# Shifting half of the features by one token: transfers in SBUF in place of products with a shift matrix (preLN mixed attention network, Trainium2)

## The chip, the cores and the metric

The kernel runs on one core of one Trainium2 chip. The core has five engines with a queue each: TensorE (PE, matrix products; PEld is its loading of the stationary operand), VectorE (DVE), ScalarE (ACT), GpSimd (POOL) and SyncE (SP, which here only issues transfers). Transfers run on 16 DMA engines beside them. Every engine works through its own queue in order and waits on semaphores for the others. The metric is the device time of one execution in microseconds.

## The reference

Eight sequences of 512 tokens with 256 features pass through four blocks: an attention with xPos rotation and a decaying product, a mixture of eight experts, a causal attention of 16 heads, and a stack of two local layers. Only the local layers are touched by the change. Cut to what matters:

```python
def shift_token(t):
    t1, t2 = jnp.split(t, 2, axis=-1)
    t2 = jnp.pad(t2, ((0, 0), (1, 0), (0, 0)))[:, :-1]
    return jnp.concatenate([t1, t2], axis=-1)

def _layer(x, wqkv, qs, ksc, wo, lg, lb, w1, b1, w2, b2):
    h = shift_token(x)
    ...                       # q, k, v; rotation; windows of 128 tokens
    x = x + o @ wo
    h = shift_token(x)
    mu = h.mean(-1, keepdims=True)
    var = h.var(-1, keepdims=True)
    h = (h - mu) / jnp.sqrt(var + 1e-05) * lg + lb
    h = h @ w1 + b1
    a, g = jnp.split(h, 2, axis=-1)
    h = a * jax.nn.gelu(g, approximate=False)
    return x + h @ w2 + b2
```

So each layer twice takes the second 128 features of every token from the token before it. The second of these shifts, the one ahead of the layernorm, is what the change is about.

## The kernel before

Rows of tokens lie on partitions. A sequence is a tile `x` of 128 partitions by 4 token tiles (t = 0 to 3) by 256 features in SBUF; all eight sequences stay there. All arithmetic is float32; each float32 product or transpose of the program is carried out as two matmul instructions, so counts in the trace are twice those of the code.

The local layers are written as 16 units (2 layers by 8 sequences). `Unit` has the steps: `flip` (transposes x to feature-major, the first shift is a change of one column there), `rows` (q and k of one token tile, with rotation), `value_rows`, `roots`, `turn` (normalise and transpose q and k), `scores`, `exponentials`, `weigh` (softmax of one token tile, four heads at a time), `flip_weights` (transposes the weights, `pt` to `pT`), `outputs` (`ov`), `project` (product with wo, and the sum into x, L997), `norm` (second shift and layernorm, L999 to L1028), `flip_normed` (transposes `hn`, L1030), `gated` (six chunks of the gated hidden layer) and `back` (product with w2, `fo`, and the sum into x at L1104).

The order is written out by hand in the loop at L1555. In iteration n the token tiles t = 0 to 3 of unit n (`u`) are attended; beside them stand steps of `ahead` (unit n+1: its flip, rows, turn), of `late` (unit n-1: norm, flip_normed, gated) and of `last` (unit n-2: back). `fill[t]` holds three lists of such steps: the first goes between `flip_weights(t)` and `outputs(t)`, the second between `outputs(t)` and the scores of the next token tile, the third behind `project(t)`. Matmuls and transposes of this part, and ACT's table loads and exponentials, keep their order of the program (`product`, L161; `transpose`, L165; `pinned`). DVE, POOL and SP get their order from the scheduler of the framework, which puts an instruction into its engine's queue where it expects it to become ready; semaphores are set by it too.

`norm` of the kernel before, at t = 0 in the first list:

```python
            sh = ps.tile([P, NT, P], F32, tag="ps", name="sh")
            for t in range(NT):
                product(sh[:, t, :], shift[:, 0, :], y[:, t, P:], start=True, stop=(t == 0))
                if t:
                    product(
                        sh[:, t, :], shift[:, 1, :], y[:, t - 1, P:], start=False, stop=True
                    )
```

`shift[:, 0]` is a matrix that moves every row one partition down, and `shift[:, 1]` one that moves the last row of the token tile before into row 0. That is 7 products per unit, into one PSUM buffer `sh` of the pool `ps` (three buffers, which `sh`, `fo`, `tp`, `qp`, `fp` and `tpq` take in turn). Statistics (L1012 to L1014) and normalisation (L1021) then read the first half of the features from x and the second from `sh`. ACT computes the inverse root as the exponential of a logarithm (L114).

SP issues in this part, in the kernel before, the loads of the second layer's weights (`wo`, `wf`, L738 to L747), and in the second layer per unit one load of the kept input (`x<-kept`, L1089) and one store of the result (`out_dram<-x`, L1106).

Of the kernel before, what the change touches and what calls it, by code (L numbers as in the profile page):

```python
# [10 lines left out]
F32 = mybir.dt.float32  # L11
# [8 lines left out]
P = 128  # L20
B, L, D = 8, 512, 256
NT = L // P
# [30 lines left out]
def forward_kernel(  # L53
# [22 lines left out]
    w2: bass.AP,  # L76
    b2: bass.AP,
    c_ident: bass.AP,
    c_shift: bass.AP,
    c_mask: bass.AP,  # L80
    c_rank: bass.AP,
    c_order: bass.AP,
# [8 lines left out]
    nc = tc.nc  # L91
# [51 lines left out]
    def layernorm(xb, dst):  # L143

        mv = moments(xb)
        standard(xb, dst, mv, rstd_of(mv, NT))
# [14 lines left out]
    def product(*args, **kw):  # L161

        tc.keep_in_program_order(nc.tensor.matmul(*args, **kw))  # L163
# [31 lines left out]
    with ExitStack() as st:  # L195
        pr1 = st.enter_context(tc.tile_pool(name="pA3", bufs=1, side="right"))
        pr2 = st.enter_context(tc.tile_pool(name="pA4", bufs=2, side="right"))
        ps = st.enter_context(tc.tile_pool(name="psA", bufs=6, space=PSUM))
# [11 lines left out]
        xs = [load_rows(0)]  # L210
# [25 lines left out]
        class Sequence:  # L236
# [6 lines left out]
            def norm(self):  # L243
                self.xn = p1.tile([P, NT, D], F32, tag="xn", name="xn")
                layernorm(xs[self.b][:, :, 1, :], self.xn)
# [232 lines left out]
        for b in range(B):  # L478
            keep = tc.keep_in_program_order
            for t in range(NT):  # L480
# [8 lines left out]
                last = (b, t - 1) if t else (b - 1, NT - 1)  # L489
# [19 lines left out]
                if b < 4 and t % 2 == 1:  # L509
# [3 lines left out]
                            out=w2_all[:, e].rearrange("p (f d) -> p f d", f=NF),  # L513
                            in_=ew2[e].rearrange("(f p) d -> p f d", p=P),
                        )
                    )
            if b == 2:
                keep(
                    nc.sync.dma_start(
                        out=rows_out.rearrange("(p s) d -> p s d", s=NS),  # L520
                        in_=c_zero[:, :D].unsqueeze(1).to_broadcast([P, NS, D]),
# [11 lines left out]
    with ExitStack() as st:  # L533
# [8 lines left out]
        number, steps = slots[0:1, :NS], slots[:, NS : NS + 32]  # L542
# [49 lines left out]
        start = chosen(need[0:1, :ne], "start")  # L592
# [110 lines left out]
        ahead = None  # L703
        for s in range(NS):
# [4 lines left out]
            ahead = (s, hT, g, c2, r)  # L709
# [8 lines left out]
    xs = [xpool.tile([P, NT, D], F32, tag=f"x{b}", name=f"x{b}") for b in range(B)]  # L718

    kept = [dram.tile([P, NT * D], F32, tag=f"kept{b}", name=f"kept{b}") for b in range(B)]  # L720
    wl = ctx.enter_context(tc.tile_pool(name="wl", bufs=1))
    masks = wl.tile([P, L + 2 * P], F32, name="masks")
    nc.sync.dma_start(out=masks, in_=c_mask)
    causal, window = masks[:, :L], masks[:, L:]
    shift = wl.tile([P, 2, P], F32, name="shift")
    rope2 = wl.tile([P, NT, 4, DH2], F32, name="rope2")
    lng_sb = wl.tile([P, DEPTH, NC], F32, name="lng_sb")
    lnb_sb = wl.tile([P, DEPTH, NC], F32, name="lnb_sb")
# [20 lines left out]

    wqkv_of = [load_qkv(0, wl)]  # L750
    layer = load_layer(0)
    nc.sync.dma_start(out=shift, in_=c_shift)
    nc.sync.dma_start(out=rope2, in_=c_rope2)
    nc.sync.dma_start(out=lng_sb, in_=lng)
    nc.sync.dma_start(out=lnb_sb, in_=lnb)
# [55 lines left out]
    class Unit:  # L811
# [172 lines left out]
        def project(self, t):  # L984
# [11 lines left out]
            y = xs[self.b][:, t, :]  # L996
            nc.vector.tensor_tensor(y, pr[:, :D], y, ALU.add)  # L997

        def norm(self):  # L999

            y = xs[self.b]
            sh = ps.tile([P, NT, P], F32, tag="ps", name="sh")
            for t in range(NT):
                product(sh[:, t, :], shift[:, 0, :], y[:, t, P:], start=True, stop=(t == 0))
                if t:
                    product(
                        sh[:, t, :], shift[:, 1, :], y[:, t - 1, P:], start=False, stop=True
                    )
            mv = lnp.tile([P, NT, 2], F32, tag="mv", name="mv")
            for t in range(NT):  # L1010
                sta = lnp.tile([P, 2, 6], F32, tag="st2", name="st2", bufs=4)
                nc.vector.bn_stats(sta[:, 0, :], y[:, t, :P])  # L1012
                nc.vector.bn_stats(sta[:, 1, :], sh[:, t, :])
                nc.vector.bn_aggr(mv[:, t, :], sta.rearrange("p a b -> p (a b)"))  # L1014
            exponentials_next()
            rstd = lnp.tile([P, NT], F32, tag="rstd", name="rstd")
            inverse_root(rstd, mv[:, :, 1], pinned=True, bias=eps)
            self.hn = d1.tile([P, NT, D], F32, tag="hn", name="hn")
            for t in range(NT):
                for c, src in enumerate((y[:, t, :P], sh[:, t, :])):  # L1020
                    nc.vector.tensor_scalar(  # L1021
                        self.hn[:, t, c * P : (c + 1) * P],
                        src,
                        mv[:, t, 0:1],
                        rstd[:, t : t + 1],
                        ALU.subtract,
                        ALU.mult,
                    )  # L1028
# [84 lines left out]
    ps = ctx.enter_context(tc.tile_pool(name="psC", bufs=3, space=PSUM))  # L1113
# [5 lines left out]
    with ExitStack() as st:  # L1119
# [373 lines left out]
        for slot in range(max(max(fill) + 1, END + 3)):  # L1493
            steps = []
            if slot < END:
                n, i = divmod(slot, UNITS)
# [6 lines left out]
            n, i = divmod(slot - 3, UNITS)  # L1503
# [7 lines left out]
            n, i = divmod(slot, UNITS)  # L1511
# [8 lines left out]
    with ExitStack() as st:  # L1520
        d1 = st.enter_context(tc.tile_pool(name="pD1", bufs=1))
        d2 = st.enter_context(tc.tile_pool(name="pD2", bufs=2))
        psb = st.enter_context(tc.tile_pool(name="psDb", bufs=2, space=PSUM))
        psa = st.enter_context(tc.tile_pool(name="psDa", bufs=1, space=PSUM))

        wqkv_of.append(load_qkv(1, d1))

        uT = d1.tile([P, NFC, L], F32, name="uT")
        nc.vector.memset(uT[:, NFC - 1, :], 1.0)

        qT = d1.tile([P, H2 // 2, L], F32, name="qT")
        kT = d1.tile([P, H2 // 2, L], F32, name="kT")

        def unit(n):
            return units[n] if 0 <= n < len(units) else None

        def steps(u, *names):

            return [(getattr(u, name), args) for name, *args in names] if u else []

        u = units[0]
        for t in range(NT):
            u.turn(t)
            if t == 0:
                for quad in range(2):
                    u.scores(0, quad)
                for quad in range(2):
                    u.exponentials(0, quad)
        for quad in range(2):
            u.weigh(0, quad)  # L1550

        for n in range(len(units) + 2):  # L1555
            u, ahead, late, last = unit(n), unit(n + 1), unit(n - 1), unit(n - 2)
            fill = [
                [
                    steps(late, ("norm",)) + steps(last, ("back", 0)),
                    steps(last, ("back", 1)) + steps(ahead, ("flip",)),  # L1560
                    steps(last, ("back", 2))
                    + steps(ahead, ("rows", 0, 0))
                    + steps(last, ("back", 3))
                    + steps(ahead, ("rows", 0, 1))
                    + steps(late, ("flip_normed",)),
                ],
                [
                    steps(late, ("gated", 0), ("gated", 1)),
                    steps(ahead, ("value_rows", 0)),
                    steps(ahead, ("rows", 1, 0), ("rows", 1, 1), ("rows", 2, 0)),  # L1570
                ],
                [
                    steps(late, ("gated", 2), ("gated", 3)),
                    [],
                    steps(ahead, ("rows", 2, 1), ("rows", 3, 0), ("rows", 3, 1)),
                ],
                [
                    steps(ahead, ("roots",)) + steps(late, ("gated", 4), ("gated", 5)),
                    steps(ahead, *(("turn", t) for t in range(NT))),
                    steps(ahead, *(("value_rows", t) for t in range(1, NT))),  # L1580
                ],
            ]
            for t in range(NT):
                then, at = (u, t + 1) if t + 1 < NT else (ahead, 0)
                if u:
                    u.flip_weights(t)
                for do, args in fill[t][0]:
                    do(*args)
                if u:
                    u.outputs(t)  # L1590
                for do, args in fill[t][1]:
                    do(*args)
                if then:
                    for quad in range(2):
                        then.scores(at, quad)
                    for quad in range(2):
                        then.exponentials(at, quad)
                if u:
                    u.project(t)
                rest = fill[t][2]  # L1600
                for i, (do, args) in enumerate(rest):
                    do(*args)
                    if i < 2 and then:
                        then.weigh(at, i)
                if then:
                    for i in range(len(rest), 2):
                        then.weigh(at, i)
            if u and u.b == B - 1 and u.l + 1 < DEPTH:
                layers.append(load_layer(u.l + 1))
# [3 lines left out]
def _constants():  # L1613
    f = np.float32
    ident = np.eye(P, dtype=f)


    shift = np.zeros((P, 2, P), f)
    shift[np.arange(P - 1), 0, np.arange(1, P)] = 1
    shift[P - 1, 1, 0] = 1  # L1620

# [32 lines left out]
    i, j = np.arange(2 * NT - 1)[None, :, None], np.arange(P)[None, None, :]  # L1656
# [24 lines left out]

    return {
        "c_ident": ident,
        "c_shift": shift,
        "c_mask": mask,
        "c_rank": rank,
        "c_order": np.ascontiguousarray(order),
# [73 lines left out]
```

## Time and profile before

| what | us |
|---|---|
| median of 3 runs (lowest, highest) | 2668.21 (2662.66, 2675.25) |
| profiled execution, its own time | 2658.87 |
| its span, first to last instruction | 2657.2 |
| PE busy (share of the span) | 2501.0 (94%) |
| DVE, ACT, POOL busy | 1553.7, 1123.8, 464.0 |
| local layers: first and last `sh` start | 1328.5, 2608.0 |
| from one `sh` of the second layer's units to the next (1930.50 to 2017.58) | 87.1 |
| one matmul instruction of `sh`, and their number | 0.275, 224 |
| granted TensorE clock, mean of the span | 0.975 |

The page of the profile gives busy times by engine and by groups of instructions; a group's mean time of one matmul holds the part in which it overlaps the next. Where a matmul's share of the elapsed time is needed, the chain of waits has it, which counts every moment once. The timeline lists instructions in order of time with the idle time ahead of them and what released them; "<-issue" is a pause without a visible cause. The DMA view lists packets (one for each contiguous piece of a transfer, and small ones that signal its end), and issues with the median time from issue to landing.

### The profile page before, as it was taken

How to read it: one execution, taken by the hardware profiler on the slowest of the kernel's cores; microseconds unless marked ns; L12 is line 12 of the kernel's file. 1: busy time of each engine (PE TensorE's matmuls, PEld its weight loads, DVE VectorE, ACT ScalarE, POOL GpSimd, SP SyncE). 2: the span in 40 equal slices, each digit the busy share in tenths (PEclk: the TensorE clock that was granted, in tenths of full speed). 3: DMA queues.
4: the chain of work that ended last, by engine and by line, in shares of the span. 5: the costliest groups of instructions: out<-in, count | busy, mean ns of one | idle time of the engine just before them, and what ended most of it. 6: DMA issues, size and time to landing. Idle time of an engine off the chain costs nothing.

```text
span 2657.2 us, 39880 instructions
## 1 busy us (share of the span) xinstructions
PE 2501.0 (94%) x14590; PEld 1606.1 (60%) x14590; DVE 1553.7 (58%) x4763; ACT 1123.8 (42%) x2504; POOL 464.0 (17%) x632
## 2 busy tenths in 40 slices
PE   8998699996999999989899999999999999999998
PEld 5666688873444444444656666666666666666665
DVE  6665322224566666656676667567656766666653
ACT  2222111112444444434555555456545554555452
POOL 1322100003333333212110011001101111111100
PEclk9999799997999999979999999999999999999999
DMA  5620576633000000001000000000001000000000
GB/s 166 167 69 32 193 229 220 207 116 112 9 17 17 17 9 17 9 11 48 1 1 1 1 1 1 1 1 1 3 7 33 1 17 17 16 10 8 17 17 24
DMA packets 69495, 122.42 MB, mean 46 GB/s; under 512 B 11870, under 2 KB 47284, under 8 KB 69044
## 3 DMA queue, kind: packets, MB, share of 16 engines
q1 hardware_dynamic: 63700, 105.31, 12.4%
q0 software_dynamic: 4096, 12.59, 1.3%
q8 instruction: 117, 1.92, 0.3%
q10 hardware_dynamic: 1504, 1.97, 0.2%
q14 instruction: 78, 0.64, 0.1%
HBM read 97.96 MB, written 29.10 MB: 48 GB/s over the span
## 4 chain that ended last, share of the span: by engine, by line
PE 83%; DVE 8%; issue 3%; DMA 2%; ACT 2%; POOL 1%; SPq 0%; DVEq 0%; POOLq 0%; ACTq 0%
PE qp L163 12%; PE fp L163 11%; PE ov L163 9%; PE sc L163 8%; PE fo L163 7%; PE pr L163 7%; PE hp L668 6%; PE sd L163 5%; PE yp L691 4%; PE tpq L166 3%; PE pt L166 3%; PE qk L163 2%; PE tp L166 2%; DVE scrap L150 2%; PE vp L163 1%
## 5 line engine op out<-in xcount | busy, mean ns | idle before, releaser
L864 POOL TENSOR_TENSOR turned<-turned,turn 128x512 f32<-128x512 f32 x128 | 163.1, 1274 | 1105.6 <-DVE turn L856 1029.5
L163 PE MATMUL qp<-wqkv,xT 128*128 128x512 f32 x768 | 350.9, 599 | 0.1
L150 DVE CUSTOM_DVE_ANT_0 scrap<-sc,masks 128x256 f32<-128x256 f32 (+1 forms) x500 | 243.5, 487 | 171.5 <-PE sc L163 153.0
L163 PE MATMUL sc<-kT,qT 64*128 64x256 f32 (+2 forms) x2024 | 314.2, 429 | 13.8 <-DVE qrow L150 11.7
L163 PE MATMUL fp<-hT,wf 128*128 128x512 f32 (+1 forms) x704 | 313.8, 595 | 6.1 <-DVE hT L1040 6.1
L1311 ACT ACTIVATE pT<-sd 128x768 f32<-128x768 f32 (+1 forms) x192 | 169.1, 881 | 237.1 <-PE sd L163 117.1
L150 DVE CUSTOM_DVE_ANT_0 prob<-sc,masks 128x256 f32<-128x256 f32 (+1 forms) x512 | 164.4, 387 | 151.3 <-PE sc L163 151.3
L923 ACT ACTIVATE prob<-prob,nmax 128x256 f32<-128x256 f32 (+1 forms) x512 | 239.1, 468 | 24.0 <-DVE nmax L150 23.4
L163 PE MATMUL sd<-qA,kT 32*128 32x512 f32 (+3 forms) x1024 | 205.9, 494 | 31.8 <-ACT pT L1311 28.6
L163 PEld LDWEIGHTS qp<-wqkv,xT 128*128 128x128 f32 x768 | 141.6, 190 | 154.3 <-issue 135.2
L163 PEld LDWEIGHTS fp<-hT,wf 128*128 128x128 f32 (+1 forms) x704 | 128.3, 189 | 158.4 <-issue 139.8
L163 PEld LDWEIGHTS sc<-kT,qT 32*128 32x128 f32 (+1 forms) x2024 | 171.1, 190 | 72.3 <-DVE qrow L150 40.1
L163 PE MATMUL fo<-wf,uT 128*128 128x256 f32 (+1 forms) x768 | 190.4, 390 | 0.0
L680 DVE TENSOR_SCALAR hT<-hp,c 128x128 f32<-128x128 f32 x156 | 54.4, 349 | 211.2 <-ACT hT L678 211.2
L678 ACT ACTIVATE hT<-hp,c 128x128 f32<-128x128 f32 x156 | 57.3, 367 | 261.1 <-PE hp L668 200.6
L163 PEld LDWEIGHTS fo<-wf,uT 128*128 128x128 f32 (+1 forms) x768 | 137.6, 189 | 46.6 <-issue 29.6
L668 PEld LDWEIGHTS hp<-gT,we 128*128 128x128 f32 x1248 | 148.1, 193 | 26.0 <-DVE hT L680 14.0
L668 PE MATMUL hp<-gT,we 128*128 128x128 f32 x1248 | 159.4, 281 | 3.3 <-DVE krow L1147 1.6
L1313 POOL TENSOR_SCALAR_AFFINE_SELECT pT<-pT 128x256 f32<-128x256 f32 x256 | 101.1, 408 | 335.4 <-ACT pT L1311 335.3
L691 PE MATMUL yp<-w_all,hT 128*128 x624 | 153.7, 380 | 0.6 <-ACT hT L678 0.6
L163 PEld LDWEIGHTS sd<-qA,kT 32*128 32x128 f32 x1024 | 83.0, 190 | 116.6 <-ACT pT L1311 62.7
L1080 DVE SCALAR_TENSOR_TENSOR uT<-fp,b_sb,ge 128x512 f32<-128x512 f32 x96 | 70.6, 747 | 137.3 <-PE fp L163 123.7
(220 smaller groups left out, 4184.2 us busy)
## 6 DMA issues: line engine op xcount, KB each, us to landing
we<-in_ew SPq DMA_DIRECT2D x39, 1024.0 KB, 5.2
g<-rows_in SPq DMA_DIRECT2D x39, 256.0 KB, 3.8
w_all<-in_ew SPq DMA_DIRECT2D x8, 1024.0 KB, 8.8
rows_out<-in_c_zero SPq DMA_DIRECT2D x1, 4992.0 KB, 42.3
c<-in_eb SPq DMA_DIRECT2D x39, 128.0 KB, 4.8
rows_out<-y SPq DMA_DIRECT2D x39, 128.0 KB, 3.2
xb<-in_x_in SPq DMA_DIRECT2D x8, 512.0 KB, 6.3
kept<-x SPq DMA_DIRECT2D x8, 512.0 KB, 3.6
```

The source lines that it names most:

```text
L150: nc.vector.tensor_tensor_reduce(out=out, in0=scores, in1=mask, scale=-1.0, scalar=-MASKED, op0=ALU.add, op1=ALU.min, accum_out=largest,)
L163: tc.keep_in_program_order(nc.tensor.matmul(*args, **kw))
L166: tc.keep_in_program_order(nc.tensor.transpose(dst, src, ident))
L668: nc.tensor.matmul(hp[:, f, :], we[:, c, f * P : (f + 1) * P], gT[:, c, :], start=(c == 0), stop=(c == NC - 1),)
L678: nc.scalar.activation(hT[:, f, :], hp[:, f, :], AF.Relu, bias=bias)
L680: nc.vector.tensor_scalar(hT[:, f, :], hp[:, f, :], bias, 0.0, ALU.add, ALU.max)
L691: nc.tensor.matmul(yp, hT[:, f, :], w2_all[:, bass.ds(e, 1), f * D : (f + 1) * D].rearrange("p a d -> p (a d)"), start=(f == 0), stop=(f = ...
L864: nc.gpsimd.tensor_tensor(own.turned[:, t, s], own.turned[:, t, s], turn, ALU.add)
L923: nc.scalar.activation(pr[:, j, lo:], pr[:, j, lo:], AF.Exp, scale=-1.0, bias=nmax[:, j : j + 1], accum_out=sums[:, j : j + 1],)
L1080: nc.vector.scalar_tensor_tensor(uT[:n, i, :], val[:n, :], b1_sb[:n, l, 0, i : i + 1], ge[:n, :], ALU.add, ALU.mult)
L1311: nc.scalar.activation(pT[:, :, :at], sc[:, :, :at], AF.Exp)
L1313: nc.gpsimd.affine_select(out=pT[:, :, a : a + P], in_=pT[:, :, a : a + P], compare_op=ALU.is_ge, fill=0.0, base=0, pattern=[[0, 2], [1, P ...
```

## The change

Each `project(t)` now ends, behind its sum into x, with one transfer or two, from SBUF to SBUF, that put the second half of the features one row lower into a tile `late`; there are two such tiles, which the units take in turn. Their row 0 of token tile 0 is set to zero once, on POOL. `norm` reads `late` where it read `sh`; its products and the matrix `shift` with its load are gone. In the loop, `norm` goes from the first list of t = 0 (ahead of `outputs(0)`, with `back(0)` behind it) to the head of the second list (behind `outputs(0)`, with `back(1)` behind it).

```diff
@@ project
             y = xs[self.b][:, t, :]
             nc.vector.tensor_tensor(y, pr[:, :D], y, ALU.add)
 
+            late = lates[self.n % 2]
+            nc.sync.dma_start(out=late[1:, t, :], in_=y[: P - 1, P:])
+            if t + 1 < NT:
+                nc.sync.dma_start(out=late[0:1, t + 1, :], in_=y[P - 1 :, P:])
+
         def norm(self):
-
-            y = xs[self.b]
-            sh = ps.tile([P, NT, P], F32, tag="ps", name="sh")
-            for t in range(NT):
-                product(sh[:, t, :], shift[:, 0, :], y[:, t, P:], start=True, stop=(t == 0))
-                if t:
-                    product(
-                        sh[:, t, :], shift[:, 1, :], y[:, t - 1, P:], start=False, stop=True
-                    )
+            y, sh = xs[self.b], lates[self.n % 2]
             mv = lnp.tile([P, NT, 2], F32, tag="mv", name="mv")
@@ forward_kernel, local layers
         nc.vector.memset(uT[:, NFC - 1, :], 1.0)
+        lates = [d1.tile([P, NT, P], F32, name=f"late{i}") for i in range(2)]
+        for late in lates:
+            nc.gpsimd.memset(late[0:1, 0, :], 0.0)
@@ the order
                 [
-                    steps(late, ("norm",)) + steps(last, ("back", 0)),
-                    steps(last, ("back", 1)) + steps(ahead, ("flip",)),
+                    steps(last, ("back", 0)),
+                    steps(late, ("norm",)) + steps(last, ("back", 1)) + steps(ahead, ("flip",)),
                     steps(last, ("back", 2))
@@ loads and constants
-    shift = wl.tile([P, 2, P], F32, name="shift")
-    nc.sync.dma_start(out=shift, in_=c_shift)
```

A transfer of the first kind moves 127 rows of 512 bytes (63.5 KB), one of the second kind a single row of 512 bytes; a unit issues four of the first and three of the second.

## Prediction

> **What bounds the kernel now.** I read the busy times of the page first, then busy time by stretch, then the chain of waits around one unit boundary, then DVE's timeline there, and last the DMA view.
>
> ```profile
> PE 2501.0 (94%) x14590; PEld 1606.1 (60%) x14590; DVE 1553.7 (58%) x4763; ACT 1123.8 (42%) x2504; POOL 464.0 (17%) x632
> ```
>
> ```profile
> 1500.00:1760.00 260.00, 258.70 (x1392) 165.86 (x1388) 170.18 (x483) 138.15 (x330) 30.58 (x24) 1.00 0.00 1
> 2020.00:2280.00 260.00, 258.70 (x1392) 165.48 (x1391) 170.80 (x483) 138.15 (x330) 35.26 (x26) 1.00 0.04 12
> ```
>
> The second fence has stretches of the local layers: start and end, length, then busy time of PE, PEld, DVE, ACT, POOL, PE's clock, DMA share and GB/s. PE is busy 258.70 of 260 us at full clock (1.00); DVE has a third of its time free, and the DMA engines are nearly idle. So here time is what PE's queue holds, and another engine's work counts only where it makes PE wait. The chain of waits counts every moment once (start, length, work):
>
> ```profile
> 1668.54 0.87 PE pt L166 x8
> 1669.42 1.56 PE sh L163 x14
> 1670.98 2.79 PE fo L163 x12
> 1673.77 1.02 PE ov L163 x16
> ...
> 1692.50 0.03 issue
> 1692.52 0.81 DVE hT L1040
> ```
>
> Pieces of PE follow each other without a gap: `sh`, the shift, is on the path with 1.56 us. The first DVE piece is `hT`, 21 us later. That is the next thing that can be late.
>
> **What goes.** 7 products per unit, 14 instructions. Their row gives 0.275 us each, 61.6 us for 224, but they overlap; the path loses 1.56 us per unit (0.111 us each), 25.0 us in 16 units. In units 2 to 15 `fo` of `back(0)` still follows `pt`, so that the copies of `pT` (DVE 0.69 us, ACT 0.58) end ahead of `ov` as now. The last norm, behind unit 15, has 11.9 us of `fo` (2608.20) ahead of the transposes of `hn` and keeps the saving too. In unit 1 there is no `back`: `ov` would directly follow `pt` and wait for the copies. Between 0 and 1.56 us; I take 0, as the copies need 1 us and stand behind a new wait. **Sum: 15 x 1.56 = 23.4 us.**
>
> Off the path: DVE reads SBUF in place of PSUM (`hn<-sh` 0.407 us, `hn<-x` 0.342: 64 x 0.065 = 4 us less), the two memsets fall into 27.6 us in which POOL idles (until 1273.83), and the load of `shift` goes from a row of loads at 607 us that nothing near waits for.
>
> **What moves.** The inverse root comes behind the copy of `oT` on ACT. With `sh` gone, `ov` ends at 1673.2 on the old scale, the copy (0.58) at 1673.9, the root (0.30 + 0.21) at 1674.4, the 8 normalisations (2.4) at 1676.8, the sum of `back(1)` at 1677.2. DVE's next work, the maxima, waits for `sc` until 1679.91 - 1.56 = 1678.35. So the move is covered with 1.1 us to spare, and `hn` is ready 13 us before its transposes. If that cover went, each us would be 1 us per unit.
>
> **What is added.** Seven issues on SP per unit, about 0.35 us each (the store of `y` takes 0.36), 2.5 us of a queue with nothing else for most of a unit. At unit 7 the `wo` load (512 packets of 1 KB, 32 per engine, 1.5 us) stands ahead of its last transfer, once. In the second layer `x<-kept` waits for the store's landing (2.9 us), and the next transfer is due some 15 us later. Nothing there.
>
> The new wait is on DVE: the statistics of `late`. In the changed kernel's queues, those of t = 1 and 2 come some 15 us behind their transfer. Those of t = 0 stand right behind the sum of `back(2)`, and those of t = 3 ahead of the copy of `pT`. DVE at t = 0 (L997 is the sum that the transfer waits for):
>
> ```profile
> 1684.02 0.42 DVE L997 TENSOR_TENSOR x<-pr,x 128x256 f32<-128x256 f32 x1
> ...
> 1685.85 0.42 DVE L1104 TENSOR_TENSOR x<-fo,x 128x256 f32<-128x256 f32 x1
> 1688.01 0.69 DVE L851 TENSOR_TENSOR turned<-qp,tab 128x512 f32<-128x512 f32 x1 [1.75 <-ACT sq L849]
> ...
> 1690.17 0.42 DVE L1104 TENSOR_TENSOR x<-fo,x 128x256 f32<-128x256 f32 x1 [0.21 <-PE fo L163]
> 1692.52 0.81 DVE L1040 TENSOR_SCALAR hT<-tp,lng_sb,lnb_sb 128x512 f32<-128x512 f32 x1 [1.93 <-PE tp L166]
> ```
>
> Behind the waiting statistics are queued the rotation of `qp` (whose PSUM buffer PE wants), the sum of `back(3)`, and `hT`, for which PE waits. The idle time in brackets is the cover: 1.75 + 0.21 + 1.93 = 3.9 us, less 0.4 for statistics and aggregate, 3.5. The transfer is issued at about 1684.55 (0.1 behind the sum, as with `y`); DVE arrives at 1686.27. So landing up to 1686.27 + 3.5 - 1684.55 = **5.2 us** after issue costs nothing; each us more costs 1 us in units 2 to 15. At t = 3 the same count (sum ends 1664.48; `pT` must be copied before `ov` at 1672.1; 0.69 and 0.4 us ahead of that) gives **6.5 us**, in 15 units.
>
> **How long does it take to land?** No SBUF to SBUF transfer is in the trace, nor one of 127 rows. The DMA view of two stretches, 2038 to 2044 (loads of 640, 42 and 1 packets of 1 KB) and 2652 to the end (a store of 512):
>
> ```profile
> DMA packets 715, 0.72 MB, mean 119 GB/s; under 512 B 31, under 2 KB 714, under 8 KB 714
> ...
> wf<-in_w SPq DMA_DIRECT2D x1, 42.0 KB
> wf<-in_b SPq DMA_DIRECT2D x1, 1.0 KB
> ```
>
> ```profile
> DMA packets 529, 0.53 MB, mean 102 GB/s; under 512 B 16, under 2 KB 528, under 8 KB 528
> ...
> q1 hardware_dynamic: 528, 0.52, 28.7%
> ```
>
> The store has 512 + 16 small packets, one for the end on each of 16 engines. The three loads have 31 = 16 + 14 + 1: a load of 42 rows used 14 engines, the one row 1. 14 is the largest number up to 16 that divides 42. For 127, a prime, that would be one engine.
>
> The Trainium skill ("DMA: Bandwidth & Descriptors", section on why a DMA increments its semaphore by 16) says just this, with 127 partitions as an example that runs on a single engine; the 31 packets agree with it, and it speaks against the change. The same page's fit, 2.0 us plus bytes over 436 GB/s, would give an estimated 2.15 us for 63.5 KB, no wait at all and the whole sum; by the one-engine rule the landing comes close to the 5.2 us.
>
> The price of a packet: 28.7% of 16 engines x 5.2 us / 512 = 46.6 ns for 1 KB; in the trace's packet records the 128 packets of 512 B that load `ident` took 27 ns each (median). The fixed part: the store `out_dram<-x` lands in 2.9 us, less 32 x 46.6 ns = 1.4; `kept<-x` in 3.6, less 8 packets of 4 KB at 159 ns (same records) = 2.3. Ends:
> - all 16 engines: 8 x 27 ns + 1.3 to 2.3 = 1.5 to 2.5 us;
> - one engine, rows at the price of 1 KB: 127 x 46.6 ns + 2.3 = 8.2 us;
> - one engine, 27 ns: 3.43 + 1.4 to 2.3 = 4.8 to 5.7 us. I take this, as the row of equal size, at its middle, 5.2 us: just hidden. At 5.7 the loss is 14 x 0.5 = 7 us.
>
> **The rivals.**
> 1. *Forecast*: landing below 5.9 us, on one engine or many. Net -23.4 us (-25 to -13). From the profiled execution (2658.87) that is 2635.5; from the median of the runs shown, which lies 9.3 us higher, 2644.8. As the result will be a median too, I give **2645**.
> 2. *The wait eats the gain*: landing 5.9 to 7.1 us. With loss = 14 x (L - 5.2) + 15 x (L - 6.5), L = 6.5 loses 18 us: net -5, 2663. For it: no margin at 5.2, and the extra read and write on one SBUF side is in no row. Against: the packets of 512 B at 27 ns.
> 3. *The transfer takes the place of the product as the bound* (slower): one DMA engine carries 127 rows one after the other at 46.6 ns. At L = 8.2 DVE loses 3.0 us at t = 0 in 14 units (42) and 1.7 at t = 3 in 15 (25), less 23.4: +44, 2712. It decides from L = 6.7 on (loss 23.4), and is slower by 0.5% from 7.1 on.
> 4. *The change doesn't do what it says*: excluded as far as PE goes, the 112 products are out of its queue. That PE's freed time is lost elsewhere needs an engine near its limit; DVE, at 170 of 260 us, isn't.
>
> The one-engine rule of the Trainium skill is what rivals 2 and 3 rest on; the 14 ends of the 42-row load bear it out, so I count on one engine with 8 in 10.
>
> **How the numbers follow.** A measurement of this kernel can tell about 0.5% (13.3 us) from no change. Case 1 has 0.68 and is faster by more than that; case 2 has 0.16 and covers within 0.5% (losses of 10 to 37 us); case 3 has 0.16. Range: below, the full 25 us off the profiled execution, and 2 us for the spread, 2632; above, into case 2 up to L = 6.8 (loss 27, net +3.5), 2672. That leaves out case 3 and a little of case 2.
>
> **What would show it.** Right: one `pt` to `fo` gap without `sh`; units 85.5 us apart in place of 87.1; `late<-x` landing at 4.8 to 5.7 us with one end packet per 127-row transfer; DVE idle ahead of `st<-late` of t = 0 by about 3 us, and PE's wait for `hT` at the 0.43 us per unit that its timeline has now. Wrong: PE waiting for `hT`, or for `pT` ahead of `ov`, by a us and more per unit (rivals 2, 3); landing near 2 us would make the one-engine step wrong without moving the time.

## The result and the profile after

| | before | after |
|---|---|---|
| median of 5 runs each (lowest, highest), us | 2668.0 (2662.66, 2675.25) | 2645.48 (2641.9, 2651.38) |
| profiled execution, its own time, us | 2658.87 | 2647.91 |
| its span, us | 2657.2 | 2646.2 |
| granted TensorE clock, mean of the span | 0.975 | 0.969 |
| one unit of the local layers (units 2 to 14), us | 87.08 | 85.51 |
| start of the local layers (first transposes of q) to the end, us | 1407.4 | 1380.8 |

The ratio of the medians is 0.9919, with a 95% interval from 0.9895 to 0.9943: the kernel is 22.5 us faster. The changed kernel, timed a second time (experiment 6), gave 0.991 (0.9884 to 0.9936).

The busy times of the page, after:

```profile
PE 2490.7 (94%) x14366; PEld 1591.7 (60%) x14366; DVE 1550.2 (59%) x4763; ACT 1123.6 (42%) x2504; POOL 465.6 (18%) x634
```

PE has 224 instructions less, 14 for each of 16 units. DVE's busy time fell by 3.5 us; the normalisations of the second half, which now read SBUF, take 0.341 us each in place of 0.408, 4.3 us less in all. The two stretches of the local layers (start and end, length, busy time of PE, PEld, DVE, ACT, POOL, PE's clock, DMA share, GB/s):

```profile
1500.00:1760.00 260.00, 258.91 (x1369) 164.01 (x1368) 173.07 (x500) 141.35 (x347) 30.64 (x24) 1.00 0.02 4
2020.00:2280.00 260.00, 258.93 (x1376) 164.47 (x1376) 171.96 (x491) 138.84 (x332) 35.36 (x26) 1.00 0.05 15
```

PE is as full as before: the 1.56 us that left its queue did not turn into a pause. The chain of waits of the changed kernel (start, length, work) shows it at one unit boundary:

```profile
1421.16 0.87 PE pt L165 x8
1422.04 2.79 PE fo L162 x12
1424.83 1.02 PE ov L162 x16
1425.85 2.98 PE fo L162 x12
...
1443.55 0.03 issue
1443.58 0.81 DVE hT L1034
```

`fo` follows `pt` directly, and `hT` is still the next thing that is late, with the same 0.03 us of "issue" ahead of it. What has changed is how near DVE is to its limit there. DVE's timeline, from the sum that the last transfer waits for to `hT` (in brackets the idle time ahead and what ended it):

```profile
1435.07 0.42 DVE L994 TENSOR_TENSOR x<-pr,x 128x256 f32<-128x256 f32 x1
...
1436.91 0.42 DVE L1098 TENSOR_TENSOR x<-fo,x 128x256 f32<-128x256 f32 x1
1440.69 0.29 DVE L1007 BATCH_NORM_STATS2 st<-late 128x6 f32<-128x128 f32 x1 [3.37 <-DMA late<-x]
...
1443.58 0.81 DVE L1034 TENSOR_SCALAR hT<-tp,lng_sb,lnb_sb 128x512 f32<-128x512 f32 x1 [0.21 <-PE tp L165]
```

DVE stands idle for 3.37 us in front of the statistics of `late`, and of the 1.93 us that it used to wait ahead of `hT` 0.21 us are left. So nearly the whole cover (the idle time of DVE that the wait can use before PE has to wait too) is used, and nothing beyond it. The transfer itself, in the DMA view of 1417 to 1423:

```profile
DMA packets 130, 0.09 MB, mean 15 GB/s; under 512 B 1, under 2 KB 128, under 8 KB 128
...
late<-x SPq DMA_DIRECT2D x1, 63.5 KB
```

One small packet, which signals an end, so one engine: the 127 rows ran on a single DMA engine. In the packet records they take 27 ns each (median) and 3.36 us together; from the end of the sum on DVE to the start of the statistics that wait for it, 5.1 to 5.3 us pass in nearly every unit, and some 0.05 us less from the issue. And the waits between 1320 us and the end (what waited and for what: us in total, times, longest):

```profile
DVE st L1007 <- DMA late<-x: 103.9, 32, 4.1
...
PE fp L162 <- DVE hT L1034: 5.7, 15, 0.7
```

DVE waits 104 us for transfers, and PE 5.7 us for `hT`, against 6.1 us before. The first number is almost all covered idle time, which costs nothing (for unit 1 see below).

**Where the 22.5 us sit.** In the profiled executions the local layers are 26.6 us shorter: counted from one unit's first transposes of q to the next's, units 2 to 14 give 13 x 1.57 = 20.4, unit 1 1.4, unit 0 0.4, and the stretch from there in unit 15 to the end, in which two layernorms fall, 4.4. Ahead of the local layers the changed kernel's profiled execution took 15.7 us more, with a lower granted clock there (0.50 against 0.84 between 290 and 310 us, for instance) and the same program but for one load. That part differs from one execution to the next (experiment 6), so the medians are the measure of the whole and the local layers that of the change. Why the median fell 4 us less than the local layers did isn't shown; that part alone varies by more.

### The profile page after: what moved, and what is told of

Its sections match the earlier page's. It is cut to its first block, busy times and chain, and to the rows that moved or that the text cites. A ratio compares the mean times of both kernels' runs of the same rounds, so it can differ in the third digit from the quotient of the medians.

```text
span 2646.2 us, 39641 instructions
## 1 busy us (share of the span) xinstructions
PE 2490.7 (94%) x14366; PEld 1591.7 (60%) x14366; DVE 1550.2 (59%) x4763; ACT 1123.6 (42%) x2504; POOL 465.6 (18%) x634
## 3 DMA queue, kind: packets, MB, share of 16 engines
q8 instruction: 115, 1.88, 0.3%
q10 hardware_dynamic: 1504, 1.97, 0.2%
## 4 chain that ended last, share of the span: by engine, by line
PE 83%; DVE 8%; issue 3%; DMA 2%; ACT 2%; POOL 1%; SPq 0%; DVEq 0%; POOLq 0%; ACTq 0%
PE qp L162 12%; PE fp L162 11%; PE ov L162 9%; PE sc L162 8%; PE fo L162 7%; PE pr L162 7%; PE hp L667 6%; PE sd L162 5%; PE yp L690 5%; PE tpq L165 3%; PE pt L165 3%; PE qk L162 2%; PE tp L165 2%; DVE scrap L149 2%; PE vp L162 1%
## 5 line engine op out<-in xcount | busy, mean ns | idle before, releaser
L846 ACT ACTIVATE sq<-qp 128x512 f32<-128x512 f32 x128 | 75.8, 593 | 175.3 <-PE qp L162 131.0
```

Source lines behind the costliest of these rows:

```text
L846: nc.scalar.activation(sq, qp, AF.Square)
```

## The experiments

**1. The 127 rows as 112 + 15.** Theory: one DMA engine carries the 127 rows, and its 5.2 us are just hidden. Rivals: the rows are spread over the engines in any case; or the wait costs something that a shorter landing gives back.

```diff
-            nc.sync.dma_start(out=late[1:, t, :], in_=y[: P - 1, P:])
+            for lo, hi in ((0, 112), (112, P - 1)):
+                nc.sync.dma_start(out=late[lo + 1 : hi + 1, t, :], in_=y[lo:hi, P:])
```

> The changed kernel with each transfer of 127 rows cut into one of 112 and one of 15 rows. Theory (rows go to as many DMA engines as divides their number: 112 to 16, 15 to 15, but 127 to one; the 5.1 us that DVE waits for are just hidden from PE): landing drops from 5.1 to about 2.5 us, DVE's wait for late, 104 us in all in the changed kernel, falls below 20 us, and PE hardly notices: units stay at 85.5 us, only unit 1 loses its wait for pT of 1.4 us; local layers (from the first transposes of turned to the end) 1379 to 1381 us after 1380.8. Rival (the wait on DVE costs PE some tenths in every unit): units of 85.0 us or less, 8 us and more saved. Rival (a transfer's time is its fixed part, whatever the rows): landing stays at 5 us.

Measured: median 2645.43 us (2634.9 to 2655.21), 0.9897 (0.9872 to 0.9922) of the kernel before beside it; units of 85.52 us. The DMA view of 1499 to 1504, and DVE's wait over the local layers:

```profile
DMA packets 158, 0.07 MB, mean 13 GB/s; under 512 B 31, under 2 KB 158, under 8 KB 158
```

```profile
DVE st L1008 <- DMA late<-x: 22.7, 28, 1.5
```

The same 127 packets of 512 bytes have 31 ends (16 for the 112 rows, 15 for the 15 rows), are through in 1.0 us in place of 3.36, and land in 2.6 us. So it was the number of rows that set the number of engines. DVE's wait falls from 104 us to 23 (a little more than the 20 expected), and the time stays: the wait was hidden, as the theory has it. Unit 1 is 1.4 us shorter, and its wait for `pT` ahead of `ov`, expected to go, falls from 1.38 to 0.35 us.

**2. No shift ahead of the layernorm.** The transfers are left out and the layernorm reads `x` unshifted.

> Leaves out the shift ahead of the layernorm altogether: norm reads the second half of the features in place, with neither products nor transfers; all else as in the changed kernel. Theory (the transfers are wholly hidden, and what the change gains is the 1.56 us of products in a unit): units of 85.5 us as in the changed kernel, unit 1 without its wait, local layers 1379 to 1381 us. Rival (transfers and their waits cost something on the path): units shorter than 85.5 by what they cost, at most the 1.0 us to which issue, queue and DVE's statistics could add up.

Measured: median 2633.15 us (2630.58 to 2642.12), 0.9856 (0.9836 to 0.9876). In the trace the units take 85.51 us and the local layers 1381.1, as in the changed kernel. The trace says that the transfers cost nothing, the median that they cost 12 us (experiments 1 and 3, timed beside this one, have 2645.43 and 2644.16); experiment 6 took this up.

**3. Transfers, layernorm at its old place.** The two lines of the order in the loop are those of before, and all else is the changed kernel.

> The changed kernel with norm back at its old place, ahead of outputs(0). Theory (the move of norm is neutral, PE's order is the same): units of 85.5 us, local layers within 2 us of 1380.8. Rival (the move keeps the root and its wait off ACT's copy of oT): ACT waits in order for the statistics of t = 3, which end 1.5 us later than without a transfer, the copy of oT comes later, and units grow by up to 0.5 us, 8 us in all.

Measured: median 2644.16 us (2638.62 to 2652.62), 0.9886 (0.9869 to 0.9902); units of 85.52 us. With transfers the place of the layernorm has no effect on the time that these runs could show.

**4. The move alone.** The kernel before, with its products, and only the order in the loop changed.

```diff
-                    steps(late, ("norm",)) + steps(last, ("back", 0)),
-                    steps(last, ("back", 1)) + steps(ahead, ("flip",)),
+                    steps(last, ("back", 0)),
+                    steps(late, ("norm",)) + steps(last, ("back", 1)) + steps(ahead, ("flip",)),
```

> The kernel before with norm at its new place alone, products kept (so sh now stands behind ov). Theory (the gain is the products' 1.56 us, the place is neutral): units of 87.1 us, local layers 1405 to 1409 us after 1407.4. Rival (part of the gain is the place): units below 87.0. Against both: sh ahead of fo of back(1) starts DVE's chain later by ov's and fo's length, 4 us, hn would be ready at about 1682 in place of 1675 of the old scale, still 10 us ahead of its transposes, but the maxima come behind it on DVE and could be late by up to 2 us in a unit.

Measured: median 2682.71 us (2667.57 to 2694.21), 1.0037 (1.0016 to 1.0057); units of 87.97 us, 0.88 more than before. Here the theory failed. The timeline behind `sh` at one boundary (rows of several engines):

```profile
1617.55 0.66 PE L166 MATMUL tp<-ident,x 128*128 128x128 f32 x4
...
1618.24 0.59 ACT L830 COPY xT<-tp 128x512 f32<-128x512 f32 x1 [1.52 <-PE tp L166]
...
1618.74 0.41 DVE L1021 TENSOR_SCALAR hn<-sh,mv,rstd 128x128 f32<-128x128 f32 x1
...
1618.88 0.66 PE L166 MATMUL tp<-ident,x 128*128 128x128 f32 x4 [0.68 <-ACT xT L830]
1619.06 0.42 DVE L1104 TENSOR_TENSOR x<-fo,x 128x256 f32<-128x256 f32 x1
```

The second transposes `tp` need a buffer of the pool `ps`, which has three. At 1618.2 one is held by `sh`, whose last reader on DVE starts at 1618.74, one by `fo`, whose reader is queued behind that (1619.06), and one by the first `tp` until ACT's copy ends at 1618.83. The copy is the first to free one, and PE has waited 0.68 us, in 13 units (8.8 us in all). In the chain of waits the whole 0.88 us sits here:

```profile
1617.62 0.60 PE tp L166 x4
...
1619.53 1.93 PE sc L163 x16
```

From `tp` to `sc` 1.91 us pass, against 1.03 in the kernel before (1677.77 to 1678.80), where the eight transposes follow each other without a break; the pieces from `pt` to `tp` take 9.23 us in both. So the move is free only because `sh` is gone: without a PSUM tile of its own, the layernorm may run late without holding a buffer. The two parts of the change belong together in this way only; experiment 3 shows that the transfers don't need the move.

**5. A later landing.** A second transfer into a spare tile, which nothing reads, is issued on SP's queue ahead of each 127-row transfer, so that the one waited for comes later: with 61 rows (a prime) and with 127. This measures the price of the disputed wait.

```diff
+            nc.sync.dma_start(out=spare[:61], in_=y[:61, P:])
             nc.sync.dma_start(out=late[1:, t, :], in_=y[: P - 1, P:])
```

> The changed kernel with one more transfer ahead of each of 127 rows: 61 rows (a prime too, so one DMA engine) into a tile that nothing reads. Order on PE, DVE, ACT and POOL is unchanged. Theory (one engine works through the rows at 27 ns; cover 5.2 us at t = 0 and 6.5 at t = 3): landing 5.15 + 61 x 0.027 = 6.8 us, loss 1.6 us at t = 0 in 14 units and 0.3 at t = 3 in 15: units of 87.4 us, 27 us more in all, about the time of the kernel before. Rival (DVE, busy for two thirds, absorbs it): units of 85.5 us, no change. Rival (other engines carry the added rows): no change either, with landing at 5.2.

Measured with 61 rows: median 2680.18 us (2669.76 to 2686.5), 1.0044 (1.0025 to 1.0063); landing 7.1 to 7.3 us behind the sum in nearly every unit, some 0.3 us later than expected; units of 87.9 us (87.4 expected), 2.4 more than the changed kernel. The whole gain is gone. PE's timeline in one unit shows where:

```profile
1514.00 1.09 PE L162 MATMUL ov<-pT,v 128*64 128x128 f32 x16 [0.73 <-DVE pT L957]
...
1533.81 0.63 PE L165 MATMUL tp<-ident,hn 128*128 128x128 f32 x4 [1.46 <-DVE turn L853]
1534.64 0.66 PE L165 MATMUL tp<-ident,hn 128*128 128x128 f32 x4 [0.21 <-DVE x L1099]
```

0.73 us ahead of `ov` (behind the transfer of t = 3) and 1.46 + 0.21 us ahead of `tp` (behind that of t = 0) make the 2.4 us. The waits name `pT`, `turn` and `x`, not the transfer: what PE waits for is the work queued on DVE behind the waiting statistics. With a landing 7.08 us after the first of the two issues, the covers are 7.08 - 1.67 = 5.4 us at t = 0 and 7.08 - 0.73 = 6.35 us at t = 3.

> The same with 127 added rows. Theory: landing 5.15 + 127 x 0.027 = 8.6 us, loss 3.4 us at t = 0 in 14 units (47) and 2.1 at t = 3 in 15 (31): units of 90.9 us, 78 us more than the changed kernel in all. Rival (the wait is absorbed): units of 85.5 us. A straight line from 0 without a threshold would give 61/127 of dose127's loss in dose61, 0.48; the two thresholds give 0.35.

Measured with 127 rows: median 2767.77 us (2762.4 to 2771.92), 1.0387 (1.0363 to 1.041); landing 8.7 to 8.9 us behind the sum in nearly every unit; units of 92.6 to 95.1 us (90.9 expected). The landing came as expected, but the loss per unit, about 7.9 us, is more than the 5.7 that the covers give. Part of PE's timeline, and the granted clock (the column behind POOL) in four stretches:

```profile
1517.91 1.39 PE L162 MATMUL ov<-pT,v 128*64 128x128 f32 x16 [2.33 <-DVE pT L957]
1519.24 4.39 PE L162 MATMUL fo<-wf,uT 128*128 128x256 f32 x12
...
1540.93 0.63 PE L165 MATMUL tp<-ident,hn 128*128 128x128 f32 x4 [3.03 <-DVE turn L853]
```

```profile
1516.00:1522.00 6.00, 4.09 (x23) 3.20 (x24) 3.05 (x12) 0.99 (x3) 0.00 (x0) 0.72 0.00 0
...
1528.00:1540.00 12.00, 9.90 (x35) 5.84 (x33) 5.00 (x14) 3.46 (x12) 0.00 (x0) 1.00 0.04 11
1540.00:1546.00 6.00, 4.86 (x25) 4.45 (x26) 6.00 (x12) 0.29 (x1) 2.54 (x2) 0.72 0.00 0
...
1606.00:1618.00 12.00, 9.67 (x65) 7.41 (x65) 3.92 (x14) 3.24 (x7) 0.00 (x0) 1.00 0.03 7
```

The pauses themselves are 2.33 + 3.03 + 0.21 = 5.6 us, what the covers give. Right behind two of them the granted clock drops to 0.72 over 6 us, and `fo`, with 12 instructions, takes 4.39 us in place of 2.95. A clock of 0.72 over 6 us is 0.28 x 6 = 1.7 us of PE's work lost each time. One or two such drops per unit make the rest: 85.5 + 5.6 + 1.7 = 92.8 us, and the eight units with one drop took 92.6 to 93.4; with two it is 94.5, and four units took 94.2 to 94.4. The longest, 95.1, has one drop of double length beside a single one.

**6. The changed kernel and the one without the shift, once more, on one chip.** To settle the 12 us of experiment 2.

> The changed kernel once more, beside the kernel that leaves the shift before the layernorm out, on one chip. Theory (the transfers and the wait for them cost no time): 2645 us, and the two medians within 6 us of each other; in the profiles, units of 85.5 us in both. Rival (the transfers cost the 12 us by which the first median of the kernel without them lay lower): this one again 10 to 14 us above the other.

> The kernel without the shift before the layernorm once more (no transfers, the layernorm reads the unshifted x), beside the changed kernel on the same chip. Theory (the transfers cost nothing): a median within 6 us of the changed kernel's, near 2640 us. Rival: 2633 us, with the changed kernel at 2645.

Measured: the changed kernel 2641.71 us (2637.89 to 2648.29), the one without the shift 2638.59 (2634.8 to 2645.26); 3.1 us apart, with ratios to the kernel before of 0.991 (0.9884 to 0.9936) and 0.9897 (0.987 to 0.9923), units of 85.51 us in both. The theory holds as far as this can tell: the 12 us did not come again, the intervals of the two ratios overlap, and of the 3.1 us nothing lies in the units. Where the 12 us came from isn't shown. It also shows how far one program varies ahead of the local layers: those began at 1265.45 us in the first profiled execution of the changed kernel and at 1256.77 in the second, which had the clock of the kernel before, 0.975, and a span of 2636.2 us, 21.0 less than before's (whose local layers began at 1249.79).

## Why the prediction was right, point by point

- **What bounds the kernel** (PE's queue in the local layers): right. PE stays busy 258.9 of 260 us, and a unit is shorter by what left the queue.
- **1.56 us per unit**: right, 1.57 measured. It was right to take the chain's share and not the 0.275 us of the row, by which a unit would have lost 14 x 0.275 = 3.9 us.
- **Which units gain**: the term that was mis-sized. 15 x 1.56 = 23.4 us was forecast, with nothing from unit 1; the local layers lost 26.6. In unit 1 PE does wait 1.4 us for `pT` ahead of `ov`, as foreseen, but a wait of 2.84 us for `prob` ahead of `pt`, which it had before, is gone. Two others there grew, by 0.6 us ahead of `tp` and 0.7 ahead of `fp`, so that PE waits 0.1 us less in all, and the unit is 1.4 us shorter. The stretch from unit 15 on gave 4.4 us in place of 2 x 1.56 = 3.1. The surplus of 1.3 us is the size of a drop of PE's clock. The kernel before has 3.41 us at a granted clock of 0.50 there, in which PE is busy for 2.72 us, so that it loses 1.36 us of work:

```profile
2576.51:2579.92 3.41, 2.72 (x10) 2.23 (x11) 1.68 (x2) 0.69 (x1) 0.00 (x0) 0.50 0.03 5
```

Neither profile of the changed kernel has such a drop at that place (125.7 us each); those of experiments 1 and 3 have one, and there the stretch took 126.9 and 127.2 us, 3.3 and 3.0 less than the 130.1 of before. Whether the change has a part in the drop's absence isn't shown. These ends vary from version to version (unit 0, unit 1 and the last stretch together were 269.1 us, 267.8 the second time, 271.5 without the shift in its second run, 275.3 before), so a single profile doesn't settle the size.
- **The move at no cost**: right, for the reason given. DVE's last sum behind the normalisations ended 1.54 us before its next work (1.1 forecast), and the old place gives the same time. What the prediction did not see is that this holds only without `sh`: with the products the move costs 0.88 us per unit.
- **Cover of 5.2 and 6.5 us**: right. Experiment 5 gives 5.4 and 6.35.
- **Landing at 5.2 us on one engine, 27 ns a row**: right, 5.1 to 5.2 us from the issue, 3.36 of them packets, so that the fixed part was 1.8 (1.4 to 2.3 forecast; the row for 16 engines has 1.3 where the working gives 1.4, without effect). That the middle of 4.8 to 5.7 was hit is in part luck: no row told where in it the landing would fall. The one-engine rule of the Trainium skill ("DMA: Bandwidth & Descriptors", section on why a DMA increments its semaphore by 16) agrees with the one end packet here and with the 31 of the split transfer. That page gives its fit for transfers issued from GpSimd, which the prediction leaves unsaid; these are issued from SP. The estimated 2.15 us that it gave isn't what these runs show: the measured landing of the 127 rows is 2.4 times as long, that of the split transfer 2.6 us.
- **The rivals**: both were real and not far. The landing of 7.1 us in experiment 5 is rival 2's upper end, and the kernel came out 0.44% slower than before; at 8.8 us it was 3.9% slower, more than the 44 us that rival 3 gave for 8.2. The formula of the rivals gives 12 us of loss against before for 7.1, and 12.0 were measured; for 8.7 from the issue it gives 59, and 99.6 were measured, as PE's clock dropped too, which the formula doesn't have. What decided was the price of a packet, 27 or 46.6 ns, and the choice of the row of equal size.
- **Seven issues on SP of 0.35 us**: mis-sized without effect. The 127 rows took 0.60 us to issue and the single row behind them 0.92 to 1.00, some 5.3 us per unit in place of 2.5, on a queue with nothing else. The single row's time is not a price of its shape: it was 0.55 us behind the split transfer, 1.8 to 2.1 with 61 rows added ahead and 3.5 with 127, so it grew with the rows queued ahead of it. The `wo` load at unit 7 put one landing off to 5.9 us, and that unit is no longer than the others.
- **The base**: the forecast of 2645 went by the median, and that it was met within 0.5 us is luck: the local layers lost 26.6 us in place of 23.4, and the second median of the same kernel was 2641.71. From its own profiled time it was 2635.5; the first profiled execution of the changed kernel, at the lower clock, took 2647.91, and the second, at the clock of before, 2637.89.

## What to carry to other kernels

Where one engine is full, the gain of taking work off it is that work's share of the chain of waits, and whether it arrives depends on the waits put in its place: count the idle time of the engine that waits, up to the piece that the full engine needs from it, and set it against the landing. The transfers of 127 and of 61 rows, both primes, ran on one DMA engine each (one end packet). Splitting the 127 rows into 112 + 15 halved the landing for one more issue, and gives back the margin though it doesn't shorten this kernel. Moving a step that held a PSUM buffer cost 0.88 us per unit here, and the same move without the buffer nothing, so a move and the removal of a buffer have to be judged together.

## What the runs showed that I had not expected

With pauses of PE of 2.3 to 3.0 us the granted clock fell, to a mean of 0.72 over 6 us, twice in one unit, while after a pause of the same 2.33 us in the next unit (ahead of 1612.19) it stayed at 1.00. With pauses of up to 1.46 us (61 rows) it stayed at 1.00 in units 2 to 14. Seen closer, each drop is 3.41 us at 0.50, which is the 1.7 us lost:

```profile
1518.57:1521.98 3.41, 3.41 (x16) 2.52 (x12) 1.58 (x7) 0.99 (x3) 0.00 (x0) 0.50 0.00 0
1542.46:1545.87 3.41, 3.41 (x17) 3.34 (x16) 3.41 (x6) 0.16 (x1) 1.27 (x1) 0.50 0.00 0
```

The drops of this run lie on a fixed grid: from 1518.57 to 1542.46 it is 7 times 3.413 us, and from there to the next, at 1634.62, 27 times. The grid tells the two pauses of 2.33 us apart. The one that ended at 1517.91 lies whole in one step of it (1515.16 to 1518.57), and the drop came at the end of that step. The other, 1609.86 to 1612.19, is cut by the grid at 1610.73 into 0.87 and 1.46 us, and none came. The pause of 3.03 us is cut by the grid at 1539.05, and what lies behind, with the 0.21 us after it, 1.88 + 0.21 = 2.09 us in one step, was followed by a drop. So it was the idle time within one step that counted, in these three cases: 2.09 and 2.33 us brought the clock down, 1.46 didn't. A wait beyond its cover can therefore cost more than its length, here up to 1.7 us more per pause. The Trainium skill ("TensorE: Matmul & The Clock Gate", "Part 1: The HAM clock gate") describes a free-running window of about 3.4 us, after one idle window of which the clock is halved. That the same pause does it in one unit and not in the next, by its place on the grid of 3.413 us, agrees with a free-running window, and 3.41 us at 0.50 with a window at half clock; that 2.09 us of pause in a window are enough is less than the page says.
